# A two-layer graph attention kernel: three of eight layer 0 tiles fetched in rows by indirect DMA instead of gathered by matmuls, and the layer norm in pairs of tiles

## The chip, the cores and the metric

The kernel runs on one core of a Trainium2 chip. The core has a matrix engine (TensorE; PE in the profile, PEld for its weight loads), three engines for elementwise work (VectorE or DVE, ScalarE or ACT, GpSimd or POOL), a queue that issues transfers (SyncE or SP) and 16 DMA engines. Each engine runs its own instructions in program order, and waits for others by semaphores. The metric is the device time of one execution in microseconds (us). The kernel before takes 2507.32 us, the median of three runs from 2503.66 to 2509.24.

## The reference

There are 16 graphs (batches, b) of 1024 nodes with 64 features, and an adjacency matrix of about nine neighbours a node with the node itself. Each batch goes through two attention layers, and a layer norm with a residual follows each:

```
# layer 0: 8 heads of 64, attention over a node's neighbours
scores = leaky_relu(q @ k.T / 8 + edge_bias[edges], 0.2), -1e9 where there is no edge
x = layernorm(x + (softmax(scores) @ v) @ Wp + bp)
# layer 1: one head, additive attention
hp = x @ lin_w.T + lin_b ;  s = leaky_relu(hp@W1.T [i] + hp@W2.T [j], 0.2)
e = s . a, -9e15 where there is no edge
x = layernorm(x + elu(softmax(e) @ hp))
```

## The kernel before

Dense attention over 1024 x 1024 pairs is avoided. Groups of GR = 8 nodes share one list of neighbours. A batch has NT = 8 tiles of 128 nodes; a tile is 16 groups, in two halves n of NQ = 8 groups q. Each group has SLOTS = 120 places: 2 x CAP2 = 112 for neighbours, found in four segments of 256 columns, and 8 for its own nodes. Attention of a tile is then over 120 places a group, with a mask for places that a node doesn't use.

**The lists.** `prepare(b)` (L308) reads the adjacency matrix, packs eight rows into one code by matmuls (`pat`, L331), and finds the WIN = 34 lowest columns of each segment by MAX8 and MATCH_REPLACE8 on DVE (`ka`, `kb`, `lst`). It writes the columns to DRAM as `col_d` (L397), the codes as `slot_d` (L408), and spreads these into `rows_s` (L413), from which `finish(b)` (L423) makes the mask. It is a generator: between its `yield`s lie pieces, 41 a batch. `Lists.place(g, k)` runs pieces at five places a step until the number is reached that PIECES and QUOTA give; `start(b + 1)` (L284) with the loads of `xs`, the diagonal and the first adjacency tiles is called within a piece of the batch before. A place with another number than the last stops at a piece that ends with "sums", so that matmuls of the lists come at the end of a step.

**The gather.** For a tile `load` (L460) copies its 2176 columns to all partitions (`cb`, 544 KB). `indicate` (L468) compares them with each partition's row number in two DVE instructions (L475): the result `f` is a matrix of ones and zeros, bf16. `gather(t, hs)` (L488) multiplies x, held as three bf16 parts `t3` that add up to the fp32 value (`thirds`, POOL), by `f`: 26 matmuls (L499) for each hs into a PSUM bank `pg`, which ACT copies to `xg` (L505). So `xg` holds the features of each group's neighbours with the features on the partitions; `own` (L481) puts the group's own nodes into its last 8 places (POOL copy, L484). `turn` (L509) transposes `xg` by 8 matmuls (L518) into `xn`, with the 120 places on the partitions, copied by ACT (L519).

**Layer 0** of tile t: `queries`, `score` (reads `xg` and the mask; DVE adds and takes the maximum, L611 to L620), `exps` (ACT, L629), `divide` (reciprocal on DVE, product on POOL, L637), `turn_weights` (PE transposes `pp`, L645), `attend` (PE, reads `xn`, L655), and for odd tiles `heads`, `rows` and `residual`, which work on a pair of tiles: the sum with `xs` goes into `y`, and `Norm.look` (L542) takes mean and variance of each tile. `end` (L697) calls `Norm.scale` (L547) once for all eight tiles: four POOL instructions, of which two have 512 columns, write `x1`. **Layer 1** has `own_rows` (POOL, L728), `project`, `weigh`, `exps`, `turn_weights`, `attend`, `rows`, `residual`; its `end` (L809) is a generator that is worked off piece by piece at the places.

**The order** is written out by hand (L883 to L941): every engine gets its instructions in the order in which the code issues them. Step g gathers tile t = g mod 8 of layer 0, scores tile g - 1, divides, turns and attends tile g - 2, and finishes tile g - 3; layer 1 follows LAG = 12 steps behind (u = g - 12). `indicate` for layer 0 is one step ahead, `load` two. Layer 0 of the next batch is set up at the end of step t = 6 (`Layer0`, with `begin`: L521), layer 1 of the batch before at the end of t = 2. `lists.place(g, 0)` stands at the beginning of a step, the others between its parts, the last at its end.

If a list overflows, a flag (`bad`) leads to a second, dense program (`all_pairs`); with this input it isn't run.

Of the kernel before, what the change touches and what calls it, by code (L numbers as in the profile page):

```python
# [22 lines left out]
GR = 8  # L23
SEG = 256
# [9 lines left out]
def kernel(  # L34
# [205 lines left out]
    nc.vector.memset(root, -0.5)  # L240
    setup.close()
# [13 lines left out]
    PIECES = 41  # L255
# [28 lines left out]
    def start(b):  # L284

        xs = dbl.tile([P, NT, D], F32, tag="xs", bufs=3, name=f"xs_{b}")
        dg = sml.tile([P, NT], I32, tag="dg", bufs=2, name=f"dg_{b}")
        diag = adj[b].rearrange("r c -> (r c)")[0 : N * N : N + 1]
        for n in range(2):
            nc.sync.dma_start(xs[sub(n), :, :], by_rows(x[b], n))  # L290
            nc.sync.dma_start(
                dg[sub(n), :], diag[n * 512 : n * 512 + 512].rearrange("(t r) -> r t", r=D)
            )
        ads = {}

        def load(k):
            hs, T = divmod(k, NT)
            if hs < 2:
                ads[k] = dbl.tile([P, 2, SEG], I32, tag="ad", bufs=4, name=f"ad_{b}_{hs}_{T}")
                nc.sync.dma_start(  # L300
                    ads[k], adj[b, ts(T, P), :].rearrange("p (n c) -> p n c", n=2)[:, :, hs * SEG : hs * SEG + SEG]
                )

        for k in range(4):
            load(k)
        started[b] = xs, dg, ads, load

    def prepare(b):  # L308
# [3 lines left out]
        xs, dg, ads, load = started.pop(b)  # L312
# [97 lines left out]

        rows_s = per.tile([P, NT, 2 * CAP2], BF16, tag="rows_s", name=f"rows_s_{b}")
# [8 lines left out]
        edges[b] = (xs, col_d)  # L420
        late[b] = (flags, dg, rows_s)

    def finish(b):  # L423

        flags, dg, rows_s = late.pop(b)
        mask = dbl.tile([P, NT, SLOTS], BF16, tag="mask", bufs=4, name=f"mask_{b}")
        nc.vector.tensor_scalar(mask[:, :, 0 : 2 * CAP2], rows_s, code, NEG, ALU.not_equal, ALU.mult)
        yield
        dgf = sml.tile([P, NT], F32, tag="dgf", bufs=2, name=f"dgf_{b}")
        nc.vector.tensor_scalar(dgf, dg, 1.0, None, ALU.is_ge)  # L430
        own = sml.tile([P, NT, GR], F32, tag="own", bufs=2, name=f"own_{b}")
        nc.vector.tensor_tensor(
            own, dgf.unsqueeze(2).to_broadcast([P, NT, GR]), own_i.unsqueeze(1).to_broadcast([P, NT, GR]), ALU.mult
        )
        nc.vector.tensor_scalar(mask[:, :, 2 * CAP2 : SLOTS], own, 0.0, NEG, ALU.is_equal, ALU.mult)
        yield
        nc.vector.tensor_scalar(dgf, dg, 2.0, None, ALU.is_ge)
        nc.vector.tensor_reduce(flags[:, 18:19], dgf, XX, ALU.max)
        fl = sml.tile([P, 1], F32, tag="fl", bufs=2, name=f"fl_{b}")
        nc.vector.tensor_reduce(fl, flags, XX, ALU.max)  # L440
        nc.vector.tensor_scalar(fl, fl, 0.5, None, ALU.is_ge)
        nc.vector.tensor_tensor(bad, bad, fl, ALU.max)
        masks[b] = mask
# [13 lines left out]
    class Tiles:  # L457
# [63 lines left out]
        def begin(self, x_):  # L521
# [4 lines left out]
            self.xT = dbl.tile([P, 512], F32, tag=f"xT{self.layer}", name=f"xT{self.layer}_{b}")  # L526
# [8 lines left out]
    class Norm:  # L535
# [11 lines left out]
        def scale(self, dst, y):  # L547
            rs = sml.tile([P, NT], F32, tag="rs", name=f"rs_{self.nm}")
            nc.gpsimd.tensor_tensor(rs, self.mv[:, :, 1], eps.to_broadcast([P, NT]), ALU.add)
            nc.gpsimd.tensor_tensor(rs, rs, root.to_broadcast([P, NT]), ALU.pow)  # L550
            nc.gpsimd.tensor_tensor(dst, y, self.mv[:, :, 0:1].to_broadcast([P, NT, D]), ALU.subtract)
            nc.gpsimd.tensor_tensor(dst, dst, rs.unsqueeze(2).to_broadcast([P, NT, D]), ALU.mult)  # L552

    class Layer0(Tiles):
        layer = 0

        def __init__(self, b):
            self.b, self.cb, (self.xs, self.col_d) = b, {}, edges[b]
            self.begin(self.xs)
            self.mx = dbl.tile([P, 2, NG // 4], F32, tag="mx", name=f"mx_{b}")  # L560
            self.y = dbl.tile([P, NT, D], F32, tag="y", name=f"y0_{b}")
            self.norm = Norm(f"0_{b}")
            self.qp, self.ls, self.den, self.w = {}, {}, {}, {}

# [125 lines left out]
        def residual(self, t):  # L690
# [3 lines left out]
            for t_ in (t - 1, t):  # L694
                self.norm.look(self.y, t_)

        def end(self):  # L697
            x1 = dbl.tile([P, NT, D], F32, tag="x1", name=f"x1_{self.b}")
            self.norm.scale(x1, self.y)
# [5 lines left out]
            return x1  # L705

    class Layer1(Tiles):
        layer = 1

        def __init__(self, b, x1):  # L710
            self.b, self.cb, self.x1, (_, self.col_d) = b, {}, x1, edges[b]
# [5 lines left out]
        def sums(self):  # L717
# [4 lines left out]
            self.u = dbl.tile([P, NT, D], F32, tag="u", name=f"u_{self.b}")  # L722
# [86 lines left out]
        def end(self):  # L809
# [13 lines left out]
            for t in range(0, NT, 2):  # L823
                norm.look(y, t)
                norm.look(y, t + 1)
                yield
            norm.scale(o, y)
            yield
# [9 lines left out]
    QUOTA = (3, 3, 5, 6, 6, 6, 6, 6)  # L838
# [7 lines left out]
    class Lists:  # L846
# [11 lines left out]
        def place(self, g, k):  # L858
            b, t = divmod(g + AHEAD, NT)
            due = PIECES * b + sum(QUOTA[:t]) + QUOTA[t] * (k + 1) // PLACES  # L860
# [11 lines left out]
    with tc.manual_schedule(engines={getattr(mybir.EngineType, e) for e in order}):  # L872
        for _ in prepare(0):
            pass
        for _ in finish(0):
            pass
        l0[0] = Layer0(0)
# [5 lines left out]
        for g in range(NT * B + LAG + 7):  # L883
# [10 lines left out]
            at(l0, g, "gather", 0)  # L894
            at(l0, g - 3, "heads")
            at(l0, g, "gather", 1)
# [14 lines left out]
            lists.place(g, 2)  # L911
            at(l1, u - 1, "weigh")
# [3 lines left out]
            at(l1, u, "gather", 1)  # L916
# [440 lines left out]
```

## Time and profile before

| | us |
|---|---|
| median of three runs | 2507.32 |
| the profiled execution's own time | 2508.74 |
| its span, first to last instruction | 2506.8 |
| busy: PE / PEld | 2308.1 / 1957.7 |
| busy: DVE / ACT / POOL | 2012.1 / 1445.2 / 912.9 |
| one batch in the middle, 8 steps | 146.46 |

All times of the trace are of one execution. A group's row names the source line, the engine, the operation, what it writes and reads, shapes and how many; behind the bar stand the busy time in us, the mean of one in ns, and the time that the engine was idle just before them, with what ended it. The ends of matmuls are modelled, so a busy PE isn't a PE at its peak. The granted clock of TensorE is 0.988 over the span. The 16 DMA engines are busy for 28.3% of the span with the kernel's one queue, in 190,052 packets and 223.49 MB; 91,492 packets have less than 512 bytes.

The steps start with the first matmul of `score` (L603). In the middle of the run they last, for t = 0 to 7, 18.4, 17.4, 20.4, 19.1, 18.4, 15.6, 17.9 and 19.2 us. The first step starts at 102 us; before it stand the weights' products and the lists of batch 0. The last 12 steps have layer 1 alone.

### The profile page before, as it was taken

How to read it: one execution, taken by the hardware profiler on the slowest of the kernel's cores; microseconds unless marked ns; L12 is line 12 of the kernel's file. 1: busy time of each engine (PE TensorE's matmuls, PEld its weight loads, DVE VectorE, ACT ScalarE, POOL GpSimd, SP SyncE). 2: the span in 40 equal slices, each digit the busy share in tenths (PEclk: the TensorE clock that was granted, in tenths of full speed). 3: DMA queues.
4: the chain of work that ended last, by engine and by line, in shares of the span. 5: the costliest groups of instructions: out<-in, count | busy, mean ns of one | idle time of the engine just before them, and what ended most of it. 6: DMA issues, size and time to landing. Idle time of an engine off the chain costs nothing. (4 is left out here: it accounts for less than half of the span.)

```text
span 2506.8 us, 110853 instructions
## 1 busy us (share of the span) xinstructions
PE 2308.1 (92%) x48706; PEld 1957.7 (78%) x48706; DVE 2012.1 (80%) x5237; ACT 1445.2 (58%) x4401; POOL 912.9 (36%) x1106
## 2 busy tenths in 40 slices
PE   5387999999999999999999999999999999999986
PEld 3376788878788887878788787888878888888864
DVE  6687879888888988888898888889888888876642
ACT  0154656656565665656566566656656665666743
POOL 1133333434334343433434343342434434243331
PEclk9998999999999999999999999999999999999998
DMA  3412332423233242323324232332423233221210
GB/s 102 122 59 89 104 103 78 133 77 116 73 102 108 78 133 80 114 73 107 103 78 133 84 109 75 106 103 78 133 86 108 81 100 106 62 92 57 66 52 18
DMA packets 190543, 230.66 MB, mean 92 GB/s; under 512 B 91492, under 2 KB 157092, under 8 KB 190052
## 3 DMA queue, kind: packets, MB, share of 16 engines
q1 hardware_dynamic: 190052, 223.49, 28.3%
q8 instruction: 384, 6.29, 1.0%
q14 instruction: 107, 0.88, 0.1%
HBM read 218.23 MB, written 5.21 MB: 89 GB/s over the span
## 5 line engine op out<-in xcount | busy, mean ns | idle before, releaser
L499 PE MATMUL pg<-f,x 128*64 128x272 bf16 (+2 forms) x13312 | 804.5, 272 | 37.4 <-DVE f L475 34.5
L499 PEld LDWEIGHTS <-x 128*64 128x64 bf16 x13312 | 662.0, 109 | 115.5 <-issue 70.4
L637 POOL TENSOR_TENSOR ls<-ls,den 128x480 f32<-128x480 f32 x256 | 285.8, 1117 | 921.1 <-DVE den L636 912.6
L475 DVE TENSOR_SCALAR f<-cb,jrow 128x2176 bf16<-128x2176 bf16 x512 | 491.6, 1001 | 0.3 <-DMA cb<-col_d 0.3
L505 ACT COPY xg<-pg 128x448 f32<-128x448 f32 x512 | 271.5, 530 | 356.1 <-PE pg L499 355.1
L629 ACT ACTIVATE ls<-ls,mx 128x120 f32<-128x120 f32 x1024 | 391.2, 386 | 4.8 <-DVE mx L620 4.8
L519 ACT COPY xn<-pt 120x512 f32<-120x512 f32 x512 | 277.3, 597 | 11.8 <-PE pt L518 7.1
L751 ACT ACTIVATE r<-pz 128x480 f32<-128x480 f32 x256 | 132.1, 568 | 247.0 <-PE pz L746 247.0
L518 PE MATMUL pt<-ident,xg 128*120 128x128 f32 x2048 | 273.9, 276 | 0.0
L484 POOL COPY xg<-xT 128x64 f32<-128x64 f32 x256 | 107.2, 426 | 387.9 <-PE pt L518 345.4
L518 PEld LDWEIGHTS pt<-ident,xg 128*120 128x120 f32 x2048 | 224.0, 137 | 27.3 <-issue 24.8
L752 DVE SCALAR_TENSOR_TENSOR r<-pz,r 128x480 f32<-128x480 f32 x256 | 155.4, 649 | 50.6 <-ACT r L751 50.6
L629 ACT ACTIVATION_READ_ACCUMULATOR ls<-ls,mx 128x1 f32 x1024 | 194.8, 190 | 0.0
L619 DVE SCALAR_TENSOR_TENSOR ls<-sc 128x480 f32<-128x480 f32 x256 | 191.5, 748 | 0.0
L620 DVE TENSOR_REDUCE mx<-ls 128x4 f32<-128x480 f32 x256 | 167.2, 653 | 8.8
L611 DVE TENSOR_TENSOR sc<-s,rowc 128x480 f32<-128x480 f32 x256 | 155.1, 647 | 22.7 <-PE s L603 21.0
L746 PEld LDWEIGHTS pz<-rw,ub 64*64 64x64 f32 x4096 | 122.6, 133 | 63.9 <-issue 58.5
L655 PE MATMUL z<-w,xn 120*64 120x64 f32 x4096 | 159.2, 227 | 4.4 <-ACT w L647 4.4
L587 DVE TENSOR_TENSOR qp<-pq,qb 128x512 f32<-128x512 f32 x128 | 87.9, 686 | 90.0 <-PE pq L586 89.8
L655 PEld LDWEIGHTS z<-w,xn 120*64 120x64 f32 x4096 | 138.4, 139 | 27.7 <-ACT w L647 19.4
L645 PE MATMUL pp<-ident,ls 128*120 128x128 f32 x1024 | 142.0, 280 | 19.3 <-POOL ls L637 16.6
L740 PE MATMUL pz<-xg,w2d 64*64 64x480 f32 x1024 | 140.4, 588 | 17.1 <-DVE sc L611 17.1
(212 smaller groups left out, 3881.1 us busy)
## 6 DMA issues: line engine op xcount, KB each, us to landing
cb<-col_d SPq DMA_DIRECT2D x256, 544.0 KB
ad<-in_adj_dram SPq DMA_DIRECT2D x256, 256.0 KB
xs<-in_x_dram SPq DMA_DIRECT2D x32, 128.0 KB
rows_s<-slot_d SPq DMA_DIRECT2D x256, 14.0 KB
out_dram<-o SPq DMA_DIRECT2D x32, 128.0 KB
col_d<-col SPq DMA_DIRECT2D x128, 4.2 KB
dg<-in_adj_dram SPq DMA_DIRECT2D x32, 2.0 KB
slot_d<-slot SPq DMA_DIRECT2D x16, 28.0 KB
```

The costliest lines, as they stand in the source:

```text
L475: nc.vector.tensor_scalar(fj.rearrange("p s n q k -> p (s n q k)"), cb.rearrange("p s n q k -> p (s n q k)"), jrow[:, j : j + 1], None, AL ...
L499: nc.tensor.matmul(pg[sub(n), :, FIRST * a_ + lo : FIRST * a_ + to], self.t3[:, k, 4 * hs + 2 * a_ + j, :], f[j][:, 2 * hs + a_, n, :, lo:to],
L505: nc.scalar.copy(dst, pg)
L518: nc.tensor.transpose(pt[:, q, :], xg[:, 4 * m + q, :], ident)
L519: nc.scalar.copy(self.xn[t][:, ts(m, 4), :], pt)
L611: nc.vector.tensor_tensor(sc, both[n], self.rowc[:, n, ts_].unsqueeze(2).to_broadcast([P, 4, SLOTS]), ALU.add)
L619: nc.vector.scalar_tensor_tensor(ls, scs[n], SLOPE, scs[n], ALU.mult, ALU.max)
L620: nc.vector.tensor_reduce(self.mx[:, n, ts_], ls, XX, ALU.max, negate=True)
L629: nc.scalar.activation(ls[:, q, :], ls[:, q, :], AF.Exp, bias=neg[:, q : q + 1], accum_out=den[:, q : q + 1])
L637: nc.gpsimd.tensor_tensor(ls, ls, den.unsqueeze(2).to_broadcast([P, 4, SLOTS]), ALU.mult)
L655: nc.tensor.matmul(zz[sub(n), q, :], xn[:, q, sub(n)], w_[n][:, q // 2, sub(q % 2)], start=True, stop=True)
L752: nc.vector.scalar_tensor_tensor(r, pz[n], SLOPE / (1.0 - SLOPE), r, ALU.mult, ALU.add)
```

## The change

Of layer 0's eight tiles, FETCHED = (2, 5, 7) are no longer gathered by matmuls. `start` copies x of the batch to a DRAM tensor `table` with one row more (row 0, for empty places; three DMAs on SP). `prepare` works out from the lists for each group and place the row in `table` (`at_s`, about seven small DVE instructions), transposes it on PE and clips it to whole numbers on DVE (`at_d`: 120 places on the partitions, one column a group). `fetch(b, t, k)` issues on POOL one indirect DMA for one group: 120 rows of 256 bytes from `table` to a half of `xf`, which has the layout of `xn`. A tile takes 16 of them, a batch 48; each of a batch's 40 places issues one or two, one to two steps ahead of their tile.

For a fetched tile `load`, `indicate`, `own` and `turn` do nothing, and `gather(t, hs)` transposes four groups of `xf` into `xg` (4 matmuls and one ACT copy). In a fetched tile's step the second half of `gather` comes ahead of `heads`; in the step behind, layer 1's second half of `gather` comes ahead of `weigh`. `Norm.scale` now takes a pair of tiles, with `look` in it: layer 0 calls it in `residual` of odd tiles, in place on `y`, and layer 1's `end` four times. `x1` is `y` itself. Some tiles have another number of buffers (mask 3, xT of layer 1 and u one, y three). PIECES is 44 and QUOTA gives a piece more to each of its last three steps. Ahead of the first tile ten places are run, with the first 12 fetches.

```
+    def fetch(b, t, k):
+        _, _, table, rows_at = edges[b]
+        if k == 0:
+            fetched[b, t] = dbl.tile([SLOTS, NQ, P], F32, tag="xf", bufs=3, name=f"xf_{b}_{t}")
+        n, q = divmod(k, NQ)
+        g = D * n + NQ * t + q
+        nc.gpsimd.indirect_dma_start(
+            out=fetched[b, t][:, q, sub(n)], out_offset=None, in_=table[:, :],
+            in_offset=bass.IndirectOffsetOnAxis(ap=rows_at[:, g : g + 1], axis=0),
+        )
...
+        def gather(self, t, hs):
+            if t not in FETCHED:
+                return super().gather(t, hs)
+            nm = f"{self.b}_{t}"
+            if hs == 0:
+                self.xn[t] = fetched.pop((self.b, t))
+                self.xg[t] = dbl.tile([P, NQ, SLOTS], F32, tag="xg0", bufs=2, name=f"xgf_{nm}")
+            pt = ps_g.tile([P, 4, SLOTS], F32, tag="g", name=f"ptf_{nm}_{hs}")
+            for q in range(4):
+                nc.tensor.transpose(pt[:, q, :], self.xn[t][:, 4 * hs + q, :], ident[0:SLOTS, 0:SLOTS])
+            nc.scalar.copy(self.xg[t][:, ts(hs, 4), :], pt)
...
+        tb = per.tile([P, NSEG, WIN], F32, tag="tb", name=f"tb_{b}")
+        nc.vector.tensor_tensor(tb, seg_at.unsqueeze(2).to_broadcast([P, NSEG, WIN]), win, ALU.subtract)
+        nc.vector.scalar_tensor_tensor(tb, who, 0.5, tb, ALU.is_ge, ALU.mult)
...
+        yield "sums"
+        pi = ps_z.tile([SLOTS, P], F32, tag="z", name=f"pi_{b}")
+        nc.tensor.transpose(pi, at_s, ident)
+        at_d = dbl.tile([SLOTS, P], I32, tag="at_d", name=f"at_d_{b}")
+        nc.vector.tensor_scalar(at_d, pi, 0.0, float(N), ALU.max, ALU.min)
...
-        def scale(self, dst, y):
-            rs = sml.tile([P, NT], F32, tag="rs", name=f"rs_{self.nm}")
...
+        def scale(self, dst, y, t):
+            two = slice(t - 1, t + 1)
+            for t_ in (t - 1, t):
+                self.look(y, t_)
+            rs = sml.tile([P, 2], F32, tag="rs", name=f"rs_{self.nm}_{t}")
...
-    QUOTA = (3, 3, 5, 6, 6, 6, 6, 6)
+    QUOTA = (3, 3, 5, 6, 6, 7, 7, 7)
+    FETCHED = (2, 5, 7)
...
         def place(self, g, k):
             b, t = divmod(g + AHEAD, NT)
+            i, todo = PLACES * t + k, 2 * NQ * len(FETCHED)
+            for j in range(todo * i // (PLACES * NT), todo * (i + 1) // (PLACES * NT)):
+                if b < B:
+                    fetch(b, FETCHED[j // (2 * NQ)], j % (2 * NQ))
...
+        for k in range(2 * PLACES):
+            lists.place(k // PLACES - AHEAD, k % PLACES)
         l0[0] = Layer0(0)
```

## The prediction

> **What bounds the kernel now.** I read the page's busy shares first, then busy time step by step, then the groups, then the timeline. A step is one pass of the loop over g; t is g modulo 8. The page:
>
> ```profile
> PE 2308.1 (92%) x48706; PEld 1957.7 (78%) x48706; DVE 2012.1 (80%) x5237; ACT 1445.2 (58%) x4401; POOL 912.9 (36%) x1106
> ```
>
> PE leads, DVE is next, POOL looks free. The engines' busy time in the eight steps of one batch, t = 0 to 7 (columns: stretch, PE, PEld, DVE, ACT, POOL, clock, DMA share, GB/s):
>
> ```profile
> 1202.90:1221.33 18.43, 17.82 (x378) 14.99 (x378) 15.13 (x42) 9.55 (x27) 4.58 (x5) 1.00 0.21 68
> 1221.33:1238.72 17.39, 17.39 (x347) 14.39 (x345) 12.22 (x26) 12.58 (x43) 6.32 (x9) 1.00 0.55 185
> 1238.72:1259.16 20.44, 18.75 (x410) 16.03 (x409) 17.97 (x51) 9.77 (x28) 10.38 (x12) 1.00 0.09 31
> 1259.16:1278.26 19.10, 17.25 (x373) 14.96 (x370) 18.64 (x45) 11.83 (x38) 6.05 (x8) 1.00 0.22 68
> 1278.26:1296.70 18.44, 17.44 (x382) 14.88 (x378) 15.91 (x43) 10.62 (x32) 3.77 (x5) 1.00 0.40 127
> 1296.70:1312.26 15.56, 15.56 (x342) 13.69 (x338) 13.27 (x32) 10.87 (x33) 3.84 (x5) 1.00 0.12 41
> 1312.26:1330.18 17.92, 17.92 (x413) 15.63 (x409) 14.54 (x36) 12.02 (x37) 5.30 (x6) 1.00 0.26 69
> 1330.18:1349.36 19.18, 18.66 (x413) 15.50 (x409) 17.25 (x44) 12.95 (x43) 16.60 (x20) 1.00 0.61 202
> sum 146.46, PE 140.79 PEld 120.08 DVE 124.93 ACT 90.20 POOL 56.85; mean PE 17.60 PEld 15.01 DVE 15.62 ACT 11.28 POOL 7.11
> ```
>
> PE fills t = 1, 5 and 6; in t = 3 DVE does (18.64 of 19.10), and in 2 and 7 it is close. So time taken from PE is worth its full size in some steps only. The groups:
>
> ```profile
> L499 PE MATMUL pg<-f,x 128*64 128x272 bf16 (+2 forms) x13312 | 804.5, 272 | 37.4 <-DVE f L475 34.5
> ...
> L637 POOL TENSOR_TENSOR ls<-ls,den 128x480 f32<-128x480 f32 x256 | 285.8, 1117 | 921.1 <-DVE den L636 912.6
> L475 DVE TENSOR_SCALAR f<-cb,jrow 128x2176 bf16<-128x2176 bf16 x512 | 491.6, 1001 | 0.3 <-DMA cb<-col_d 0.3
> ```
>
> POOL waited 912.6 us for one small DVE result: it has room, but it works between DVE results. L475 lasts from 755 (median 780) to 1800 ns, and the timeline shows why:
>
> ```profile
> 1199.31 1.41 POOL L552 TENSOR_TENSOR o<-o,rs 128x512 f32<-128x512 f32 x1
> 1199.74 1.56 DVE L475 TENSOR_SCALAR f<-cb,jrow 128x2176 bf16<-128x2176 bf16 x1
> ...
> 1217.35 1.47 DVE L475 TENSOR_SCALAR f<-cb,jrow 128x2176 bf16<-128x2176 bf16 x2
> ```
>
> One takes 1.56 us when it starts inside a POOL instruction; two take 1.47 us where POOL is idle. The first ends 0.58 us after POOL's.
>
> **The gather, removed and replaced.** 16 batches x 3 tiles = 48 fetched tiles. Each drops 52 matmuls of L499: 804.5/256 = 3.14 us of PE, 150.8 in all. The 8 transposes of L518 (1.07 us in the timeline) leave step t+1 and 8 of almost the same shape enter step t. So a fetched step loses 2.1 us of PE and the next 1.1; fetched are 2, 5, 7. Both L475 of the tile go from DVE in step t-1: 2 x 1.00. ACT loses two copies of 530 ns and exchanges two of 597 for two like L751 (568): -1.1 us, not on the path (58% busy). POOL loses L484, 426 ns. SP loses 48 loads of 544 KB (26.7 MB) and gains three table writes a batch at 0.6 us an issue; those come over a batch ahead, so no fetch waits for them.
>
> **The index work.** About seven small DVE instructions a batch, sized like L393 (301 ns), L401 to L403 (172 to 227) and L782 (288): 1.6 us. One PE transpose, 0.3. QUOTA moves a piece each into t = 3, 4 and 5; a piece there is one MAX8 and its replacement, 0.94 us.
>
> **The steps after**, each the larger of PE and DVE with the 0.3 to 0.6 us that this engine idles in it now: t = 0: PE 16.7, -1.1; t = 1: PE 17.4, 0; t = 2: PE 16.7, but DVE's 18.0 stays, -2.1; t = 3: PE 16.2, but DVE 18.64 + 0.94, +0.5; t = 4: PE 17.4, DVE down to 14.9, of PE's 1.0 idle 0.4 goes, -0.4; t = 5: PE 13.5, but DVE 14.2, -1.4; t = 6: PE 16.8, -1.1; t = 7: PE 16.6, but DVE 17.25, -1.3. Sum -6.9 a batch, of 9.6 that PE loses. Over 15.5 batches (the first runs at part load): -107.
>
> **The fetches on POOL.** 16 indirect DMAs a tile, 768 in all, 6 a step. No row shows one. From below: SP issues the rows_s DMAs 16 in 5.54 us, 0.35 each. From above: the slowest small POOL instruction, the power of L550, 1.86 us. I take 1.1, the middle, which is also nearest to an ordinary POOL instruction (L637, 1.12). A batch's POOL time becomes 56.9 + 48 x 1.1 + 3 = 113 of about 139 us, 81%. Each place issues one or two, so those queued behind (divide, own, own_rows) are 1 to 2 us late; "divide 1" ends at 1250.3 and its reader L645 starts at 1253.35, so that is covered. At 0.35 POOL is at 77 us; at 1.86 it is at 149, more than a batch takes now.
> The lock that L475's rows show may also hold a fetch off while L475 runs: 26 x 0.77 = 20 us a batch at most, which would put POOL at 133, still under 139.
> [...]
>
> **The lock on DVE.** With POOL 39% busy the 1001 ns of L475 lie 0.23 above the unlocked 0.77. If a fetch locks as an arithmetic instruction does, twice the POOL time adds another 0.25 to the 26 left: 6.5 us a batch; if it locks nothing, 0. A third of them stand in DVE-bound steps; I take +2 a batch, +31.
>
> **The norm by pairs.** Per norm, 0.2 + 1.86 + 1.06 + 1.2 = 4.3 us becomes four times (0.2 + power + two of 128 columns at about 0.42). For two columns instead of eight the power is between 0.2 (L549) and 1.86; I take 0.5. So 6.2, at most 11.6: +2 a norm, 4 a batch, in the 3 above together with the missing L484. In even steps the chain (1.5, at most 2.9 us) comes ahead of "divide 1" on POOL, whose lead over L645 is 3.1: covered, but then by nothing more. The last chain before the end shortens from 4.3 to 1.5: -3 in the tail.
>
> **Start.** Two steps of places move ahead of the first tile: 12 fetches (13 us of POOL) ahead of the thirds, and 8 conversions L324 with their loads (94.1 to 101.5 now) ahead of the first indicator; SP issues the tile's first load after those. The first step waits about 9 us longer, less later. With the tail, +6.
>
> **Fewer buffers** (xT1, u, mask, y for x1): their last readers are queued in the step of the next writer or earlier, 0. That u and xT1 then wait for POOL's own_rows and own is a cost only if POOL lags.
>
> **Sum.** -107 + 31 + 6 = -70 on the profiled span of 2506.8: 2436.8. That execution's own time is 2508.7, 1.9 around the span; the median of the three runs is 1.4 less, which makes 2437.
>
> **Rivals.** 1. POOL becomes the bound, slower. The place is POOL's queue in every step, the price the POOL time of a fetch; it decides at (146.5 - 59.9)/48 = 1.80 us, the lock's share included. At 1.86 a batch takes 149: 16 x 2.7, and 14 at the start, 2565. With a quarter of the lock's 20 us on top 154: 2640; with all of it 169: 2880. [...] Against: POOL's 90 idle us a batch.
> [...]
> 2. The lock makes DVE the bound: the full 6.5 us on the path eat the 6.9: 2480 to 2520; other locked work (L619 varies from 0.62 to 0.78 us in the timeline) decides the side. For: L475's spread. Against: a fetch need not read a tile as arithmetic does.
> 3. DVE slips over step bounds and the full PE time counts: the span 2506.8 - 151 + 5 for 16 index transposes + 6: 2367. For: DVE has 12.2 of 17.4 us in t = 1. Against: scores and exps tie the engines within a step.
> 4. "divide 1" late by 1 us in four steps a batch, +64: 2500.
>
> **How the numbers follow.** Forecast (2400 to 2470) 0.36; rival 3 0.16; rival 2 0.10 and rival 4 0.06, both around no change: of their 0.16, 0.08 faster, 0.03 same, 0.05 slower; rival 1 0.32. Faster 0.60, same 0.03, slower 0.37; runs spread 0.22%, so 0.2% is about what can be told from no change. The range goes from the full PE gain, 2360, to rival 1 with a quarter of the lock, 2640; it leaves out the upper 0.13 of rival 1 and 0.06 below. The forecast's own range is 2400 to 2470.
>
> **What the profile after would show.** L499 at 10816 matmuls and some 655 us; L475 416 times, its mean 1.0 to 1.25 us; POOL at 70 to 80% with 768 DMA instructions of about 1.1 us; steps 2, 5 and 7 shorter by 1.3 to 2.1 us, step 3 no shorter. Wrong would be: POOL over 95% or PE waiting for ls, own or ub of POOL in every step (rival 1 or 4), L475 over 1.3 us (rival 2), or PE waiting for fetched rows, which leave a full step ahead.

## The result and the profile after

The changed kernel takes 2672.98 us (median of four runs, 2670.73 to 2677.04) beside 2505.49 for the kernel before in the same runs: a ratio of 1.068, 95% interval 1.064 to 1.071. It is 167 us slower; forecast were 2437 us in a range of 2360 to 2640, and the time lies above the range too. The profiled execution has a span of 2675.3 us and a mean granted clock of 0.940, where the kernel before has 0.988.

From the page of the changed kernel: the busy shares, the clock granted to TensorE in tenths by fortieths of the span, and four groups.

```profile
PE 2280.1 (85%) x46226; PEld 1908.4 (71%) x46226; DVE 1956.6 (73%) x5261; ACT 1394.3 (52%) x4305; POOL 1774.4 (66%) x2213
...
PEclk9987999999999999899999989999999899999997
...
L609 POOL DMA_INDIRECT xf<-table,at_d x768 | 820.1, 1068 | 221.8 <-issue 194.8
L538 PE MATMUL pg<-f,x 128*64 128x272 bf16 (+2 forms) x10816 | 658.2, 275 | 6.5 <-DVE f L514 4.2
...
L514 DVE TENSOR_SCALAR f<-cb,jrow 128x2176 bf16<-128x2176 bf16 x416 | 373.3, 938 | 1.6 <-DMA cb<-col_d 1.6
...
L736 PE MATMUL pp<-ident,ls 128*120 128x128 f32 x1024 | 154.3, 293 | 88.3 <-POOL ls L728 86.3
```

The parts came in as expected: 768 fetches of 1.07 us, GpSimd at 66% and not full, and the gather's matmuls down by 146 us (804.5 to 658.2). Yet TensorE's busy time fell by 28 us only, and its idle time (span less busy) rose from 199 to 395 us. The first difference is the clock. By the mean granted clock 0.060 x 2675 = 161 us of full-speed time are missing, against 0.012 x 2507 = 30 before: 131 us more. So some 196 us of new idle time and some 130 us lost to a lower clock stand against 146 us of matmuls saved.

Eight steps in the middle show where. Three of them, t = 2, 5 and 7, and the sum of all eight (columns as in the prediction: stretch, its length, busy time of PE, PEld, DVE, ACT, POOL, clock, DMA share, GB/s):

```profile
1175.00:1195.30 20.30, 18.29 (x367) 15.49 (x365) 17.71 (x47) 11.51 (x36) 12.12 (x16) 0.92 0.29 80
...
1231.10:1254.60 23.50, 17.56 (x302) 13.94 (x301) 12.73 (x28) 12.22 (x43) 14.01 (x19) 0.85 0.64 183
...
1272.80:1299.60 26.80, 18.83 (x367) 14.91 (x365) 16.73 (x44) 13.68 (x46) 24.43 (x37) 0.94 0.34 97
...
sum 158.80, PE 137.55 PEld 116.34 DVE 122.30 ACT 84.72 POOL 109.57; mean PE 17.19 PEld 14.54 DVE 15.29 ACT 10.59 POOL 13.70
```

A batch takes 158.8 us for 146.5, but most steps are as long as before. A few are very long, and which ones changes from batch to batch: over the full batches in the middle the longest step is t = 6 (28.2 us), then 5, then 7, then 5 and 6 again, and near the end 4 (25.6 us). The step of 23.50 us has 302 matmuls that keep TensorE busy for 17.56 us; the same step before had 342 in 15.56. That is the clock, 0.85 over the step.

The chain of waits of the changed kernel, the lists of TensorE and VectorE (us in total, times, longest):

```profile
PEld pp L736 <- POOL ls L728: 99.4, 49, 5.7
...
DVE ab L346 <- DMA ad<-in_adj_dram: 73.8, 61, 5.0
PE pt L868 <- ACT e L862: 65.3, 42, 5.6
...
PE po L762 <- DVE sc L702: 60.5, 33, 6.3
```

The kernel before has 20.2, 36.7, about 1 and 27.7 us in these rows, and none of more than 4.3 us. Two long steps show what the rows stand for. In the first, VectorE's conversions for the lists (L346) stand ahead of the scores' sum (L702), and they wait for an adjacency tile that SP issues behind 16 DMAs of `rows_s`. From the timeline of SP's queue, then DVE, then TensorE (start, length, instruction, count; in brackets the idle time ahead of it and what ended it):

```profile
609.92 5.53 SPq L449 DMA_DIRECT2D rows_s<-slot_d  x16
...
615.94 18.60 SPq L322 DMA_DIRECT2D ad<-in_adj_dram  x8
```
```profile
621.30 0.43 DVE L346 TENSOR_SCALAR ab<-ad 128x512 bf16<-128x512 int32 x1 [4.64 <-DMA ad<-in_adj_dram]
...
622.89 1.22 DVE L702 TENSOR_TENSOR sc<-s,rowc 128x480 f32<-128x480 f32 x2
```
```profile
623.60 2.54 PE L762 MATMUL po<-zT,wvp 64*64 64x128 f32 x32 [6.08 <-DVE sc L702]
```

In the second, the step of 26.8 us (t = 7), GpSimd works with no pause over 0.3 us from 1270.7 on: layer 1's last sum, two fetches, a pair of layer 1's norm, the cut of x into thirds, a fetch, another norm pair, and then the division for which TensorE waits:

```profile
1286.31 1.16 POOL L592 TENSOR_TENSOR rs<-rs,root 128x2 f32<-128x2 f32 x1
...
1288.28 1.93 POOL L728 TENSOR_TENSOR ls<-ls,den 128x480 f32<-128x480 f32 x2
```
```profile
1289.32 2.05 PE L736 MATMUL pp<-ident,ls 128*120 128x128 f32 x8 [5.17 <-POOL ls L728]
```

So after the result there were two theories. A: single late links (adjacency loads, norm pairs ahead of the division, layer 1's order) stall TensorE, and stalls cost half clock behind them. B: GpSimd's load itself sets the steps.

### The profile page after: what moved, and what is told of

Read it like the earlier page. It is cut to its first block, busy times and chain, and to the rows that moved or that the text cites. A ratio compares the mean times of both kernels' runs of the same rounds, so it can differ in the third digit from the quotient of the medians.

```text
span 2675.3 us, 106739 instructions
## 1 busy us (share of the span) xinstructions
PE 2280.1 (85%) x46226; PEld 1908.4 (71%) x46226; DVE 1956.6 (73%) x5261; ACT 1394.3 (52%) x4305; POOL 1774.4 (66%) x2213
## 4 chain that ended last, share of the span: by engine, by line
PE 50%; DVE 26%; POOL 12%; DMA 4%; issue 3%; ACT 3%; SPq 1%; POOLq 0%; ACTq 0%; DVEq 0%
PE pg L538 14%; PE pt L557 4%; DVE f L514 4%; POOL xf L609 3%; PE pz L828 3%; PE z L746 3%; PE pq L677 3%; DMA ad<-in_adj_dram 3%; PE pp L736 3%; PE pz L834 3%; PE po L762 3%; PE pa L879 3%; PE s L694 2%; DVE lst L399 2%; DVE sc L702 2%
## 5 line engine op out<-in xcount | busy, mean ns | idle before, releaser
L609 POOL DMA_INDIRECT xf<-table,at_d x768 | 820.1, 1068 | 221.8 <-issue 194.8
L538 PE MATMUL pg<-f,x 128*64 128x272 bf16 (+2 forms) x10816 | 658.2, 275 | 6.5 <-DVE f L514 4.2
L538 PEld LDWEIGHTS <-x 128*64 128x64 bf16 x10816 | 545.8, 110 | 72.6 <-issue 34.4
L514 DVE TENSOR_SCALAR f<-cb,jrow 128x2176 bf16<-128x2176 bf16 x416 | 373.3, 938 | 1.6 <-DMA cb<-col_d 1.6
L544 ACT COPY xg<-pg 128x448 f32<-128x448 f32 x416 | 219.4, 531 | 296.2 <-PE pg L538 294.8
L558 ACT COPY xn<-pt 120x512 f32<-120x512 f32 x416 | 226.3, 595 | 24.8 <-PE pt L557 21.6
L557 PE MATMUL pt<-ident,xg 128*120 128x128 f32 x1664 | 234.8, 287 | 0.0
L736 PEld LDWEIGHTS pp<-ident,ls 128*120 128x120 f32 x1024 | 114.1, 143 | 120.5 <-POOL ls L728 99.4
L702 DVE TENSOR_TENSOR sc<-s,rowc 128x480 f32<-128x480 f32 x256 | 155.3, 648 | 59.0 <-PE s L694 58.2
L591 POOL TENSOR_TENSOR rs<-mv,eps 128x2 f32<-128x2 f32 x128 | 28.5, 223 | 255.3 <-DVE den L727 247.0
L738 ACT COPY w<-pp 120x512 f32<-120x512 f32 x256 | 140.0, 590 | 97.8 <-PE pp L736 94.3
L346 DVE TENSOR_SCALAR ab<-ad 128x512 bf16<-128x512 int32 x256 | 119.4, 504 | 74.3 <-DMA ad<-in_adj_dram 73.8
```

The lines of the kernel that those rows point to most:

```text
L514: nc.vector.tensor_scalar(fj.rearrange("p s n q k -> p (s n q k)"), cb.rearrange("p s n q k -> p (s n q k)"), jrow[:, j : j + 1], None, AL ...
L538: nc.tensor.matmul(pg[sub(n), :, FIRST * a_ + lo : FIRST * a_ + to], self.t3[:, k, 4 * hs + 2 * a_ + j, :], f[j][:, 2 * hs + a_, n, :, lo:to],
L544: nc.scalar.copy(dst, pg)
L557: nc.tensor.transpose(pt[:, q, :], xg[:, 4 * m + q, :], ident)
L558: nc.scalar.copy(self.xn[t][:, ts(m, 4), :], pt)
L609: nc.gpsimd.indirect_dma_start(out=fetched[b, t][:, q, sub(n)], out_offset=None, in_=table[:, :], in_offset=bass.IndirectOffsetOnAxis(ap=r ...
```

## The experiments

All times are medians of four runs (E17: ten). The runs went to five chips: E1 to E4 to one, E5 to E12 to a second, E13 to E16 to a third, E17 and E18 to one each. The kernel before takes 2501 to 2506 us on every one of them.

### One part undone at a time: E1 to E4

E1 has the number of pieces that the lists really have. `prepare` yields 42 times and `Lists` once more behind it, which makes 43 pieces a batch, while the changed kernel's PIECES and QUOTA count 44:

```
-    PIECES = 44
+    PIECES = 43
-    QUOTA = (3, 3, 5, 6, 6, 7, 7, 7)
+    QUOTA = (3, 3, 5, 6, 6, 6, 7, 7)
```

> The changed kernel with PIECES 43 and QUOTA (3, 3, 5, 6, 6, 6, 7, 7): prepare has 43 pieces a batch, so that with 44 the lists run ahead by one piece more in every batch and the first conversions of the next adjacency matrix pile up at one place. Theory A (stalls of single queues, each followed by a stretch of PE at half clock): the waits of DVE for the adjacency loads (73.8 us) fall to about the 37 of before, PE's waits for sc (54.9 + 13.1 in the middle) to about 41, and the time falls by about 80 to 2595 us. Theory B (POOL's load by itself is the bound): no change, 2673 us within 10.

E2 has layer 1's second half of `gather` behind the load in every step:

```
-            if (g - 1) % NT in FETCHED:
-                at(l1, u, "gather", 1)
...
-            if (g - 1) % NT not in FETCHED:
-                at(l1, u, "gather", 1)
+            at(l1, u, "gather", 1)
```

> The changed kernel with layer 1's second half of gather always behind indicate and load, as before the change. Theory A: the second half of gather is the cover of the chain weigh, exps, turn_weights; without the move PE's wait for exps (L868, 60 us in the middle) nearly goes, some 10 to 20 us come back as a wait for r ahead of weigh, and the time falls by 40 to 80 us to about 2610. Theory B: no change, 2673 us within 10.

E3 has the norm over eight tiles at once again, in `end` of both layers (layer 0's part of the edit):

```
-            self.norm.scale(self.y, self.y, t)
+            for t_ in (t - 1, t):
+                self.norm.look(self.y, t_)
...
+            self.norm.scale(self.y, self.y)
```

> The changed kernel with the norm over all eight tiles at once again, at the places of before, in place on y. Theory A: the norm of a pair stands ahead of divide 1 on POOL; without it PE's wait for ls (L736, 51 us in the middle, 86 in all) falls below 20, and the time falls by 60 to 90 us to about 2600. Theory B: POOL has 4 us a batch less of about 110, the time falls by 5 to 15 us.

E4 fetches no tile; all the rest of the change stays:

```
-    FETCHED = (2, 5, 7)
+    FETCHED = ()
```

> The changed kernel with FETCHED empty: all tiles gathered by matmuls in the old order; the table, the index work, the norm by pairs, the buffers and PIECES 44 stay. Theory A: PE's 146 us of work come back, POOL has room again, the drift of the pieces stays: 2520 to 2570 us, above before, with waits for adjacency loads of 50 us or more. Theory B: all of the loss is the fetches on POOL, so 2505 to 2515 us as before.

Measured: E1 2875.72 us (ratio 1.149, 1.143 to 1.156), E2 2973.70 (1.187, 1.183 to 1.191), E3 2952.99 (1.178, 1.173 to 1.182), E4 2615.32 (1.044, 1.041 to 1.047). Neither theory had that. In each of E1 to E3 the wait that the edit aimed at went away: adjacency loads from VectorE's longest waits in E1, layer 1's exponentials from TensorE's in E2 (65 to 20 us), the division's in E3 (86 to 17 us). But another thing came: short gaps of TensorE behind which the profile has no releaser, inside runs of matmuls. Those of over 0.3 us with `issue` behind them, between 300 and 2800 us of the trace, number 244, 271 and 225, where the changed kernel has 6 and E4 has 8. The timeline of E1, TensorE and then GpSimd:

```profile
362.23 0.28 PE L694 MATMUL s<-mask,rep_q 64*64 64x120 bf16 x3 [0.32 <-issue]
362.97 0.22 PE L694 MATMUL s<-mask,rep_q 64*64 64x120 bf16 x1 [0.47 <-issue]
...
363.78 0.39 PE L538 MATMUL pg<-f,x 128*64 128x272 bf16 x3 [0.35 <-issue]
364.52 0.51 PE L538 MATMUL pg<-f,x 128*64 128x272 bf16 x5 [0.35 <-issue]
```
```profile
362.28 0.98 POOL L609 DMA_INDIRECT xf<-table,at_d  x1 [0.30 <-issue]
363.57 0.98 POOL L609 DMA_INDIRECT xf<-table,at_d  x1 [0.31 <-issue]
```

Here TensorE stops about twice per fetch. E4 is a plain result: 110 us of the loss are there without any fetch, more than theory A had (2520 to 2570), and theory B (no more than 2515) falls for these 110.

### The changed kernel again, all three parts undone, and the parts without fetches: E5 to E8

E8 is the changed kernel unedited, E5 has the edits of E1, E2 and E3 together, E6 is E4 with E1's 43 pieces, E7 is E4 with E3's norm.

> The changed kernel itself, unedited, beside the others. E1, E2 and E3, each of which undid one part and kept the fetches, came out 200 to 300 us above the changed kernel, with short TensorE gaps behind no releaser that the changed kernel's profile does not have (some 230 to 270 of over 0.3 us against 6). Theory C (the fetches have a second, slower course that depends on the execution or the chip and not on the edit): this run shows the gaps too, 2850 to 2980 us. Theory D (each edit brings the gaps itself, for instance by where it sets the fetches against TensorE's work): this run gives 2673 us +- 10 and 6 gaps again.

> All three edits of E1 to E3 together, fetches kept: 43 pieces of preparation, layer 1's gather behind the load in every step, the norm over eight tiles. Theory C: like the run of the changed kernel in this call, with less of the waits that each edit took away (15 to 80 us below it). Theory D: 2850 to 3000, like E1 to E3, since each edit brings the gaps.

> No tile fetched, and 43 pieces of preparation for 43 in its lists, so that a batch ends its preparation with its steps. Of the 110 us that E4 lost without any fetch, theory A's first cause is that the lists of 44 with 43 pieces drift a piece a batch, so that adjacency loads collide with VectorE's conversions (76 us of waits for them in E4 against 37 before): 2530 to 2560 us and waits for adjacency loads of 35 to 45 us. The rival, that the table, the indices and the norm by pairs cost it: 2600 to 2620.

> No tile fetched and the norm over eight tiles at once, 44 pieces. If the norm by pairs (102 us more of powers on GpSimd, ahead of the softmax divisions) carries E4's loss: 2530 to 2560 us. If the drift of the lists carries it: 2600 to 2640, and the waits for adjacency loads stay at 70 to 80 us.

Measured: E8 2680.38 us (1.072, 1.069 to 1.076), E5 2538.51 (1.014, 1.012 to 1.015), E6 2541.09 (1.015, 1.013 to 1.017), E7 2601.00 (1.039, 1.036 to 1.042). E8 and E5 have 10 and 1 of the short gaps. The three edits of E1 to E3 bring none together, so theory D falls for E5. Without fetches, 43 pieces take off 74 us and the whole norm 14. The wait behind the 74, E4's row and E6's:

```profile
DVE ab L346 <- DMA ad<-in_adj_dram: 76.3, 60, 4.8
```
```profile
DVE ab L346 <- DMA ad<-in_adj_dram: 35.7, 33, 2.7
```

With 44 counted for 43, the lists run a piece further ahead in every batch, so their conversions move from step to step and meet SP's other DMAs. That fits the longest step's wandering; in E9 below, with 43 pieces, it is t = 7 in every batch from the third on. At 43 the row is about where it was before the change (36.7 us). TensorE's totals show what a wait is worth: of the 76 us between the spans of E4 and E6 (2618.7 and 2542.9), 41 are idle time of TensorE and 35 are busy time more for the same 48722 matmuls (2356.3 and 2321.5), at a mean granted clock of 0.967 and 0.986.

### One part kept at a time, and E1 on another chip: E9 to E12

E9 is E1's kernel. The others start from E5 and bring one part of the change back: E10 the 44 pieces, E11 the norm by pairs, E12 the changed order of layer 1's `gather`.

> The kernel of E1 once more (43 pieces, all else as changed), since E5, which undoes E1's part and two more, has none of the gaps that E1 had. Theory C (a slower course of the fetches that came with the chip or the moment, not with the edit): about 2590 us, the changed kernel's 2680 less the 74 that the same edit took off without fetches (E4 to E6). Theory D (the edit brings the gaps): 2876 us again, with some 270 short TensorE gaps.

> E5 with 44 pieces for 43 again: fetches, norm over eight tiles, layer 1's gather behind the load. Theory A says the drift of the lists is worth what it was without fetches (74 us): 2612 us +- 15, with waits of VectorE for adjacency loads back at 70 us or more. The rival that the three parts only hurt together: 2545 us or less.

> E5 with the norm by pairs again, ahead of the softmax divisions on GpSimd. Without fetches it was worth 14 us (E4 to E7); with GpSimd at 66 to 70% theory A says 30 to 60 us: 2570 to 2600, with TensorE waiting some 50 us for the divided ls. If the pairs cost no more beside the fetches than without them: 2553.

> E5 with layer 1's second half gather ahead of the weights and the load again in the steps after a fetched tile. In the changed kernel TensorE waits 55 us for layer 1's exponentials in these steps (28 in E5): theory A says 27 us and some half clock, 2565 to 2590. If the order is what the fetched steps need: 2500 to 2535, faster than E5.

Measured: E9 2604.91 us (1.040, 1.038 to 1.042), E10 2620.65 (1.049, 1.047 to 1.051), E11 2630.86 (1.051, 1.049 to 1.053), E12 2522.98 (1.009, 1.008 to 1.011). The same program took 2875.72 us as E1 and 2604.91 as E9, and has 244 and 2 gaps. So the gaps go with the chip (or with what else differed between the two runs), not with an edit, and E1 to E3 can't be used as sizes. One group shows it, E1 and then E9:

```profile
L538 PE MATMUL pg<-f,x 128*64 128x272 bf16 (+2 forms) x10816 | 701.3, 279 | 46.7 <-issue 42.9
```
```profile
L538 PE MATMUL pg<-f,x 128*64 128x272 bf16 (+2 forms) x10816 | 659.3, 275 | 5.1 <-DVE f L514 4.6
```

On the second chip the parts have clear prices. 44 pieces: 75 us (E8 less E9) and 82 (E10 less E5). The norm by pairs: 82 (E9 less E12) and 92 (E11 less E5), for 14 without fetches. TensorE's wait for the division, E9 and then E12:

```profile
PE pp L736 <- POOL ls L728: 101.7, 26, 5.5
```
```profile
PE pp L729 <- POOL ls L721: 28.5, 19, 4.4
```

Most of the difference lies in one step of the eight. Over twelve batches in the middle E9's step t = 7 takes 26.0 us on average, E12's 21.0; TensorE waits for the division in E9 there and in no other step, 5.5 us a batch. All four pairs of layer 1's norm fall into t = 7, where GpSimd also cuts x into thirds. One such step of E9, in which GpSimd pauses only for the 0.2 to 0.3 us ahead of a fetch:

```profile
1236.10:1261.70 25.60, 18.74 (x369) 15.34 (x365) 14.42 (x41) 12.86 (x43) 23.46 (x35) 0.93 0.44 145
```

The changed order was held to cost; it gains: 16 us (E12 against E5) and 26 (E9 against E11). Theory A was wrong there. Nothing here is faster than the kernel before.

### What the fetches are worth, the start, and the pace: E13 to E18

E12 is still 22 us above the kernel before with 146 us of matmuls less. E15 is E12 without fetches (`FETCHED = ()`). E13 reduces the loop ahead of the first step to its fetches, and sets it behind layer 0's first load and indicators:

```
-        for k in range(2 * PLACES):
-            lists.place(k // PLACES - AHEAD, k % PLACES)
         l0[0] = Layer0(0)
...
         l0[0].own(0)
+        for k in range(2 * PLACES):
+            lists.rows(k // PLACES - AHEAD, k % PLACES)
```

`rows` holds the fetches of `place`. E14 is E13 with a number of fetches for each step of the lists, which stand two steps ahead of g:

```
+    PACE = (8, 0, 8, 8, 8, 0, 8, 8)
...
-            i, todo = PLACES * t + k, 2 * NQ * len(FETCHED)
-            for j in range(todo * i // (PLACES * NT), todo * (i + 1) // (PLACES * NT)):
+            at_t = sum(PACE[:t])
+            for j in range(at_t + PACE[t] * k // PLACES, at_t + PACE[t] * (k + 1) // PLACES):
```

E16 is E14 with `QUOTA = (3, 2, 5, 8, 6, 5, 7, 7)`.

> E12 with the loop ahead of the first step reduced to its fetches and set behind layer 0's first load and indicators; the six pieces of batch 1's preparation that the loop also ran go back into the first step. In E12's profile the first scores start at 117.7 us against 102.3 in the kernel before, and VectorE's conversions of these pieces (93.3 to 101.4, waiting for adjacency loads) stand ahead of the first query product. Theory: 10 to 15 us less, 2508 to 2513. Rival, that the late start is the index chain's (table, transposed indices) and not the pieces': 2518 to 2525.

> E13 with an uneven pace: eight fetches in each of six steps and none in the two steps whose windows show GpSimd at 19.2 of 21.0 us and 16.8 of 18.6 (the steps with the cut into thirds and the norms). Theory A (the even pace makes single steps late on GpSimd; the fetches' price hides elsewhere): the two steps lose 2 and 1 us of 16 batches, 30 to 45 us less than E13: 2465 to 2485, faster than before. Theory B' (what eats TensorE's 146 us is VectorE, at 79%, which the pace doesn't touch): 2500 to 2515, as E13.

> E12 with no tile fetched: what is left against the kernel before is the table, the index arithmetic with its transpose, and the loop ahead of the first step. By the single steps (E6 less the 14 of E7 against E4): 2527 us +- 6, so the fetches themselves would be worth only 4 us in E12 for 146 us less TensorE work. If the fetches earn what TensorE is spared beyond the stalls seen: 2560 or more.

> E14 with the preparation's pieces moved a little, from the two steps in which VectorE is busy 18.2 us to the one in which it is busy 11.4 (quota 3, 2, 5, 8, 6, 5, 7, 7 for 3, 3, 5, 6, 6, 6, 7, 7). Theory B' (VectorE sets these steps): 10 to 30 us less than E14. Theory A: no more than 5 us to either side.

Measured: E13 2859.84 us (1.143, 1.141 to 1.146), E14 3046.74 (1.216, 1.213 to 1.220), E16 3074.98 (1.229, 1.227 to 1.231), with 202, 240 and 226 gaps: again a chip with gaps, and none of the three times tells what it was to tell. E15, on the same chip, has 7 gaps and takes 2526.64 us (1.011, 1.009 to 1.012). That closes a table without fetches: 2615 (44, pairs), 2541 (43, pairs), 2601 (44, whole), 2527 (43, whole). The two parts add up there, 74 and 14. The fetches themselves are worth +65 us with 44 and pairs (E8), +64 with 43 and pairs (E9), and -4 with 43 and the whole norm (E12), which the intervals don't tell from nothing.

Where the 146 us go in E12 is seen first in TensorE's totals beside E15's: it is busy for 2213.0 us against 2317.0, 104 less, and idle for 306 against 205, 101 more. Almost all that it is spared comes back as waits. The two rows of E12 that grew most, which E15 has with 1.1 us and not at all:

```profile
PE pt L863 <- ACT e L857: 49.1, 41, 1.6
PE pq L670 <- ACT xgf L642: 25.5, 32, 1.3
```

The first is layer 1's exponentials, the second ScalarE's copy of a fetched tile's transposes. Waits for the scores' sum ahead of `heads`, for the division and for VectorE's sum of the queries grow by 16, 13 and 11 us, and the one for the scores' sum ahead of `project` goes (16 us). Then step by step. A batch in E12, t = 1 to 7 and 0:

```profile
1242.00:1259.80 17.80, 17.52 (x353) 14.48 (x349) 11.41 (x24) 12.62 (x43) 13.50 (x17) 1.00 0.59 193
1259.80:1280.00 20.20, 18.31 (x370) 15.51 (x369) 17.17 (x54) 9.90 (x27) 11.39 (x11) 0.92 0.12 40
1280.00:1298.60 18.60, 16.47 (x367) 14.33 (x365) 18.19 (x42) 10.72 (x37) 16.77 (x20) 1.00 0.58 156
1298.60:1318.10 19.50, 17.79 (x383) 15.06 (x381) 16.45 (x45) 10.39 (x31) 10.35 (x12) 1.00 0.15 44
1318.10:1332.90 14.80, 14.21 (x297) 11.99 (x296) 14.38 (x41) 10.61 (x34) 10.13 (x12) 1.00 0.11 17
1332.90:1349.70 16.80, 16.80 (x402) 14.84 (x401) 13.75 (x29) 10.91 (x35) 10.96 (x12) 1.00 0.34 90
1349.70:1370.70 21.00, 17.46 (x369) 14.04 (x365) 18.21 (x44) 12.56 (x43) 19.18 (x21) 1.00 0.57 183
1370.70:1388.00 17.30, 16.07 (x373) 13.94 (x372) 14.95 (x42) 8.60 (x25) 13.47 (x16) 1.00 0.19 47
```

and E15, t = 4, 5 and 7 and the sum:

```profile
1292.60:1311.20 18.60, 17.60 (x384) 15.05 (x380) 16.58 (x46) 10.42 (x32) 3.77 (x5) 1.00 0.44 129
1311.20:1327.00 15.80, 15.80 (x340) 13.79 (x339) 14.23 (x41) 10.89 (x35) 3.77 (x5) 1.00 0.05 11
...
1345.00:1363.80 18.80, 18.56 (x413) 15.40 (x410) 17.14 (x44) 12.62 (x43) 16.40 (x20) 1.00 0.62 199
...
sum 146.10, PE 141.07 PEld 120.47 DVE 125.95 ACT 89.56 POOL 57.05; mean PE 17.63 PEld 15.06 DVE 15.74 ACT 11.20 POOL 7.13
```

E12's eight add up to 146.0 as well. t = 5 and 6 gain about 1 us each, as TensorE has less to do. t = 7 gives 2.2 back. There VectorE has no entry in its list of waits, and GpSimd is busy for 19.18 us with no pause of over 0.3 us: both are full. In E12's timeline of that step two conversions, which take 0.4 us each where GpSimd is quiet, take 3.03 us together beside a fetch with the division close behind it:

```profile
1359.65 3.03 DVE L346 TENSOR_SCALAR ab<-ad 128x512 bf16<-128x512 int32 x2
```
```profile
1359.43 0.99 POOL L602 DMA_INDIRECT xf<-table,at_d  x1 [0.18 <-issue]
1360.45 1.93 POOL L721 TENSOR_TENSOR ls<-ls,den 128x480 f32<-128x480 f32 x2
```

The six conversions of this step take 5.41 us there. Sorted by what GpSimd did meanwhile, E12's 256 conversions last 426 ns on average beside a fetch alone, 451 beside other GpSimd work alone, and 1110 beside both. A long instruction meets more of its neighbours, so a part of this is the sorting; but over all 256 the mean is 611 ns in E12 and 441 in E15. So a fetch by itself doesn't hold VectorE up. That it makes GpSimd's arithmetic follow without a pause, which VectorE's instruction then waits out, fits the timeline; no run tests it alone.

E14 was run once more as E17, and E18 follows it with `PACE = (7, 2, 6, 8, 3, 4, 10, 8)`.

> The kernel of E14 once more. E13, E14 and E16 ran on a chip where every kernel with fetches shows the short TensorE gaps of E1 to E3 (E15, without fetches, shows none there), and nearly all of the gaps begin within 1.4 us of the start of a fetch. If this run has them too, the course of the fetches differs by chip and E14 can't be sized: over 2900. If it runs without gaps, as E5 and E9 to E12 did: theory A 2465 to 2485; theory B' (VectorE, which the pace doesn't touch, eats TensorE's gain) 2500 to 2515.

> E17 with the fetches spread by what GpSimd has free in each step of E12's windows: 7, 2, 6, 8, 3, 4, 10, 8 in place of 8, 0, 8, 8, 8, 0, 8, 8. E17's step that fell from 21.0 to 19.7 us keeps two fetches; the step in which eight fetches stood ahead of layer 0's norm and made it 22 to 23.5 us (20.2 in E12, with four) gets three. Theory A: that step returns to about 20, the others stay: 2 us a batch and some half clock, 2475 to 2495, faster than before. Theory B' (each step's length is set by the chain from scores to heads over four engines, whatever GpSimd does): 2505 to 2515. On a chip with the short TensorE gaps: over 2800, and nothing is told apart.

Measured: E17 2510.14 us (1.0025, 1.0010 to 1.0040), E18 2528.28 (1.011, 1.010 to 1.013), with 2 gaps and 1. E17 is the best kernel with fetches, and still not faster than the kernel before; theory A (2465 to 2485) falls. Of its gain on E12 a part is the start: the first scores' matmul is at 104.8 us, at 117.7 in E12, and at 102.3 before, but the eight steps from there take 5.4 us more than E12's. E15, with the six pieces of batch 1 ahead of the first step and no fetches, has it at 114.6, and E13, whose start can be read in spite of its gaps, at 107.9; so of the 13 us some 10 go with the pieces and 3 with the fetches. From the third batch on E17's steps take 7.7 us less than E12's. Steps t = 2, 3 and 7 of E17:

```profile
1244.10:1267.50 23.40, 19.91 (x366) 16.39 (x365) 18.96 (x61) 9.88 (x27) 15.05 (x14) 0.85 0.17 48
1267.50:1284.40 16.90, 15.87 (x369) 13.94 (x365) 14.52 (x35) 10.89 (x37) 14.42 (x18) 1.00 0.57 155
...
1334.60:1354.30 19.70, 17.54 (x369) 14.11 (x365) 15.01 (x42) 12.55 (x43) 18.72 (x24) 1.00 0.63 192
```

Where most fetches were taken out (t = 3 and 7) the steps are 1.7 and 1.3 us shorter, and over the run VectorE's 5261 instructions take 1885.5 us for 1995.6 in E12. But in t = 2 layer 0's norm stands behind them, and TensorE waits for its result (L591) 31.5 us in 15 places. E18 spreads them by GpSimd's free time, and t = 2 is at 20.5 us, but t = 3 and 7 are back at 19.4 and 20.6, and so is VectorE's busy time at 1977.2. Theory A (2475 to 2495) falls here, and E18 lies above B' (2505 to 2515) too; 7 of its 18 us over E17 come behind layer 0's last scores, and why is open. What the two paces show is a trade: in one order the norm pays, in the other VectorE. Whether a third order wins was not tried.

## Why the prediction was wrong

**The parts that held.** A fetch costs 1.068 us for 1.1 taken, with another 0.25 us between two (194.8 us of idle time in 759 places). The 1.1 was the middle between 0.35 and 1.86, so that it came so near is partly luck. GpSimd has 109.6 us a batch for 113 forecast: it does not fill up over a batch, as rival 1 would have it. The gather's matmuls went to 658.2 us for 655. L514's mean, 938 ns, even fell from 1001, below the 1.0 to 1.25 forecast.

**GpSimd was costed by the batch and not by the step.** This is the first of the steps that failed. "Against: POOL's 90 idle us a batch" is a sum over eight steps, and the working's own row of t = 7 had GpSimd busy for 16.60 of 19.18 us. Six fetches of 1.07 us, each with 0.25 us ahead of it, make 24.5 there, more than the step had; the changed kernel's t = 7 that is shown above has GpSimd busy for 24.43 of 26.80 us. The chain of the norm was checked against "divide 1" in even steps, where layer 0's pairs stand, and there it is covered, as forecast: E9 has no wait for the division in any even step of its middle batches. The four pairs of layer 1 all fall into t = 7 and were checked nowhere; TensorE waits 5.5 us a batch for the division behind them. So rival 1 came true in one step of eight. Rival 4 named the wait, with 1 us in four steps a batch and 64 us in all; it measured 82 to 92 us beside the fetches and 14 without them, so its size was near for another reason. Of the 89 us between the spans of E9 and E12, 55 are idle time of TensorE and 34 are more busy time for the same matmuls.

**The pieces were read from QUOTA alone.** The working has "QUOTA moves a piece each into t = 3, 4 and 5", 0.94 us a piece. Not counted was how many pieces the lists have: 43, for 44. That is 74 to 82 us, with or without fetches, the largest single price beside the pairs, and nothing in the working stood for it. Its wait (adjacency loads) is one that the profile before already had, at 36.7 us.

**The start.** With the tail it was +6. In E12 the loop ahead of the first step brings the first scores 13 us later than in E17, and E17 pays 5.4 us of these back in the eight steps that follow.

**The steps' sum of -107.** Each step was taken as the larger of TensorE's and VectorE's busy times plus a small idle time. With the pieces, the norm and nothing else in the way (E12 against E15) the fetches are worth -4 us. From the third batch on E12's steps do take 11.8 us less than E15's, but its first scores are 3.1 and its first eight steps 8.7 us longer. The steps that TensorE filled, t = 5 and 6, gave about 1.0 each for 1.4 and 1.1 forecast. Those in which VectorE was near did not: t = 2 was forecast at -2.1 and came out at -0.2, t = 7 at -1.3 and came out at +2.2, t = 4 at -0.4 and came out at +0.9. With 104 us of TensorE's work gone its waits grew by 101, the one for layer 1's exponentials above all. The likely reading is that the gather's matmuls had also filled the time in which other engines' chains ran, which busy times alone can't show.

**The lock.** "If a fetch locks as an arithmetic instruction does": it doesn't (in the changed kernel L514 takes 789 ns beside a fetch alone, 777 beside nothing and 886 beside other GpSimd work alone). Those that meet both a fetch and other GpSimd work take 1298, but the mean of all fell. So the +31 is not seen where it was placed; the longer conversions of E12, in t = 7 above all, stood in no term. The other way round, L514 does hold up fetches, by little: the 133 that start inside one take 1.22 us on average, the 539 that meet none 1.02. That is under 2 us a batch, where the working had 20 at most and the sum none.

**The clock was in no term.** Between 300 and 2300 us TensorE's clock is never halved in the kernel before; in the changed kernel it is, in 34 stretches of 3.4 us or a multiple of that, 195 us in all. A long stall so costs more than itself. E12 shows the smallest case, three windows of 3.0 to 3.4 us around a wait of 1.56 us for the scores:

```profile
1259.00:1262.00 3.00, 3.00 (x60) 2.12 (x58) 2.02 (x6) 1.91 (x10) 2.17 (x3) 1.00 0.34 100
1262.00:1265.40 3.40, 1.71 (x37) 1.24 (x36) 3.33 (x13) 0.79 (x3) 1.10 (x1) 1.00 0.04 9
1265.40:1268.80 3.40, 3.20 (x48) 2.77 (x48) 1.73 (x3) 1.24 (x6) 0.14 (x1) 0.50 0.02 5
...
```

TensorE is busy for half of the second window, and the third runs at clock 0.50. A window that was half idle, around one wait of 1.56 us, was enough there. Not every such wait does it. In the changed kernel all 20 stalls of over 2.5 us between 300 and 2300 us have half clock behind them, but 14 of the 34 from 1.5 to 2.5 us, and in E12 8 of 32 (1.5 to 1.8 us). What the stretches have in common is the share: in the 3.41 us ahead of each one TensorE was busy for at most 48% in the changed kernel and 57% in E12, and no full-speed window on the same grid with less than 46 and 52% went without.

**The sum.** From E8's 2680 us: 75 for the pieces, 82 for the pairs and 13 for the start and the pace together lead to E17's 2510, where the fetches' gain and its price cancel, 5 us above the kernel before in its own runs. Left open: why t = 4 lost 0.9 us in E12, and the cause of the gaps.

## What to carry to other kernels

When work leaves the busiest engine, cost what its new carrier does to the instructions queued behind it, step by step, rather than to that engine's total: GpSimd at 66% over the run was full in one step of eight, and that step lost some 80 us. Ask too which waits the work that leaves had covered. Count the things that a pace is built on (here 43 pieces for 44), since a schedule that drifts by one finds its collisions in turn. And price a stall of TensorE at itself plus the half clock that the trace shows behind it: in the changed kernel all 20 stalls of over 2.5 us had it, and 14 of the 34 from 1.5 to 2.5 us, for 3.4 us or a multiple of that.

## What was unexpected in the hardware

On two of the five chips named above, every kernel with fetches (six runs, E1 to E3, E13, E14, E16) took 2860 to 3075 us, with 202 to 271 TensorE gaps of mostly 0.3 to 0.5 us that no semaphore explains; on the others none did, and E4 and E15, without fetches, ran undisturbed on those two. The same program took 2876 and 2605 us (E1, E9), and 3047 and 2510 (E14, E17). In E13 all 202 such gaps began within 1.4 us behind the start of a fetch; so near to one lies some 40% of the time. The gaps are not the whole of it: in E1 they come to 131 us over the run, where its span is 263 us longer than E9's. The durations of fetches, of DMA packets and of the instruction loads are alike in both (in E1 and E9 medians of 1.02 and 1.03 us a fetch, means of 57 and 56 ns a packet, 1.07 us an instruction load). That the gaps go with the chip is what these runs show; why, they don't.
